# Inverse roots by Newton steps on GpSimd, and the interval layer's right products on two row tiles

## The chip, the cores and the metric

The kernel runs on one core of a Trainium2 chip. The metric is the device time of one execution in microseconds, taken as the median of several runs; one more execution was profiled.

## The reference

Input `x` is a batch of 4 images of 32x32 pixels with 16 channels. Three pre-activation layers of one kind and one of another are applied, each as `x = x + layer(gn(x))`, where `gn` is a group norm with 8 groups of 2 channels:

```python
def _gn(v, G=8, eps=1e-5):
    g = v.reshape(B_, H_, W_, G, C_ // G)
    m = jnp.mean(g, axis=(1, 2, 4), keepdims=True)
    s = jnp.var(g, axis=(1, 2, 4), keepdims=True)
    return ((g - m) / jnp.sqrt(s + eps)).reshape(v.shape)
...
# the three conv layers (L0, L1, L3)
first = jnp.einsum('ijyx,byxc->bijc', Msq, inputs)
diff = jax.nn.relu(inputs[:, None, None] - shifted)   # shifted: a 3x3 convolution for every pixel
second = jnp.einsum('ijyx,bijyxc->bijc', Wsq, diff)
return first - second
...
# the interval layer (L2), between the second and the third conv layer
r = interval_pooling(a, 'max') and interval_pooling(a, 'min'), side by side
ft = einsum('bikd,dh->bikh', f, Wf);  rt = einsum('bkjd,dh->bkjh', r, Wr)
f = max over k of sigmoid(ft + rt + b)    # twice, then a last sigmoid(f @ W2 + b2)
```

The convolution in a conv layer has its own 3x3 kernel for each of 1024 pixels and 16 output channels. That is nearly all of the arithmetic.

## The kernel before

The two halves of the batch (`g` = 0, 1; two images each) and the three conv layers make six phases, numbered in the order (layer 0, g 0), (layer 0, g 1), (layer 1, g 0) and so on. A phase has 8 chunks of 128 pixels, and a chunk has 32 steps: 16 channels times 2 images. There are 1536 steps. One step makes one PSUM tile `pc` of 128 pixels by 1024 positions:

- `first_part` (products at L627, tiles `ib` and `ia`) writes it, and ScalarE scales it at L663.
- `second_part` of the step before is issued after that (products at L627, tiles `iyz` and `im`), and then VectorE reduces that tile into one column at L680 (`junk`, the line that frees the tile).

So TensorE's order is first part of step n+1, second part of step n, first part of step n+2, and so on. The PSUM pool holds four pairs of banks, and `pc` tiles take them in turn. A product contracts 64 rows, and the two halves of a tile use two row tiles of TensorE, the partitions 0 to 63 and 64 to 127, one bank of the pair each.

Two other strands are woven into the steps, and the order on each engine is that of the program text, since each engine works through its own queue.

The generator `prep_parts` prepares the weights, one unit of four channels in 8 steps: VectorE takes the upper bits (L203, `upper_w`, which reads `raw` after L214), ScalarE scales and copies (L175, L236, L240), GpSimd (POOL in the profile) subtracts and adds and moves quarters (L237, L238, L241, L243, L245) and subtracts an identity from the next unit's `raw` (L214). Then SP's queue issues the transfer of `parts` (L251) and the load of a `raw` two units ahead (L110).

The generator `behind(phase)` does all that the next phase needs: the group norm, the images in the arrangement of the taps, the first terms `pf` (L425) and the interval layer. Each `yield n` in it gives the number of steps until it is resumed; `yield IDLE` waits for a step in which `prep_parts` allows it.

`group_norm` sums on VectorE, spreads the totals over the partitions (`totals`; its last instruction is the transpose to `whole_v...` at L337), takes the root on ScalarE (L358) and the reciprocal on VectorE (L360), and multiplies on GpSimd (L361, into `xn` for a conv layer and `xi` for the interval layer). Ahead of it a Sqrt of one element (`spare`, L353) loads ScalarE's table. There are eight norms: six named `c` for the conv layers and two named `i` for the interval layer. Afterwards VectorE transposes the result (L375 for `xn`, L508 for `xi`).

`interval_layer` fills a table `r` of 64 rows by 33x33 by scans and selects (the last select is L538), and then in each of two `step`s needs a left product (L548, `ps_l`) and a right product (L561, `ps_r`). `right_side` makes the right product in three blocks of 11 values of `k`, with 352, 231 and 110 columns. Each block has a PSUM tile of its own, and a copy by ScalarE into `rt` (L564) and one step lie between two blocks. Each `step` ends in a Sigmoid, ahead of which a Sigmoid of one element (L591) loads the table.

Of the kernel before, what the change touches and what calls it, by code (L numbers as in the profile page):

```python
# [8 lines left out]
F32 = mybir.dt.float32  # L9
F32R = mybir.dt.float32r  # L10
I32 = mybir.dt.int32
AF = mybir.ActivationFunctionType
ALU = mybir.AluOpType
AX = mybir.AxisListType

P = 128
B, H, C = 4, 32, 16
NG = 2
GB = B // NG
GC = GB * C  # L20
NL = 3
NP = H * H
# [16 lines left out]
T1 = H + 1  # L39
NQ = 4  # L40
# [4 lines left out]
def net_kernel(ctx: ExitStack, tc: tile.TileContext, x, xq, xi, convs, iv_w, iv_b, out):  # L45
# [26 lines left out]
    nc = tc.nc  # L72
    ctx.enter_context(tc.manual_schedule())

    const = ctx.enter_context(tc.tile_pool(name="const", bufs=1))
    wpool = ctx.enter_context(tc.tile_pool(name="wpool", bufs=2))
    work = ctx.enter_context(tc.tile_pool(name="work", bufs=1))
# [5 lines left out]
    def bank_pair(name):  # L83
        return psum.tile([P, 2, 512], F32, tag="ps", name=name)

    def bank(name):
        return bank_pair(name)[:, 0]
# [10 lines left out]
    IDLE = 0  # L98
# [55 lines left out]
    spare = const.tile([1, 1], F32, name="spare")  # L154
    nc.gpsimd.memset(spare, 0.0)
    eps = const.tile([P, 1], F32, name="eps")
# [152 lines left out]
    def pair_view(ap):  # L309
        return ap.rearrange("p t (g s) -> p t g s", s=2)  # L310

    def group_norm(g, name, dst, gap):


        def sums(src):
            nc.vector.tensor_reduce(
                part[:, : GC // 2], src.rearrange("p t (g s) -> p g t s", s=2), axis=AX.XY, op=ALU.add
            )

        def totals(name):  # L320

            turned = work.tile([P, 32], F32, tag="turned", name=f"turned_{name}")
            nc.vector.transpose(turned, part)
            by_quarter = work.tile([32, 4], F32, tag="by_quarter", name=f"by_quarter_{name}")
            for q in range(4):
                nc.vector.tensor_reduce(
                    by_quarter[:, q : q + 1], turned[32 * q : 32 * q + 32], axis=AX.X, op=ALU.add
                )
            yield gap
            total = work.tile([P, 32], F32, tag="total", name=f"total_{name}")  # L330
            for q in range(4):
                nc.vector.tensor_reduce(
                    total[32 * q : 32 * q + 32, 0:1], by_quarter, axis=AX.X, op=ALU.add
                )
            yield gap
            whole = work.tile([P, 32], F32, tag="whole", name=f"whole_{name}")
            nc.vector.transpose(whole, total[:, 0:1].to_broadcast([P, 32]))  # L337
            return whole[:, : GC // 2]

        sums(X[g])  # L340
        yield gap
        m = yield from totals(f"m{name}")
        mean = work.tile([P, GC // 2], F32, tag="mean", name=f"mean_{name}")
        nc.gpsimd.tensor_scalar_mul(mean, m, 1.0 / (2 * NP))
        xc = work.tile([P, NT, GC], F32, tag="xc", name=f"xc_{name}")
        nc.gpsimd.tensor_tensor(pair_view(xc), pair_view(X[g]), spread(mean), ALU.subtract)
        sq = work.tile([P, NT, GC], F32, tag="sq", name=f"sq_{name}")
        nc.gpsimd.tensor_tensor(sq, xc, xc, ALU.mult)
        yield 4
        sums(sq)  # L350
        yield gap
        yield IDLE
        nc.scalar.activation(spare, spare, AF.Sqrt)  # L353
        v = yield from totals(f"v{name}")
        yield 2
        yield IDLE
        rstd = work.tile([P, GC // 2], F32, tag="rstd", name=f"rstd_{name}")
        nc.scalar.activation(rstd, v, AF.Sqrt, bias=eps, scale=1.0 / (2 * NP))  # L358
        yield 2
        nc.vector.reciprocal(rstd, rstd)  # L360
        nc.gpsimd.tensor_tensor(pair_view(dst), pair_view(xc), spread(rstd), ALU.mult)  # L361
        yield 3

# [54 lines left out]
    def first_terms(layer, mt):  # L418


        sums = bank_pair(f"pf_{layer}")
        for g in range(NG):
            for pt in range(NT):
                for j in range(4):
                    nc.tensor.matmul(  # L425
                        sums[32 * j : 32 * j + 32, g, :256],
                        lhsT=xns[g][:, pt, :], rhs=mt[:, pt, j, :],
                        start=pt == 0, stop=pt == NT - 1, tile_position=(0, 32 * j),
                    )
        ft = work.tile([P, NG, NT * GC], F32, tag="fs", name=f"ft_{layer}")  # L430
        for g in range(NG):
            nc.vector.transpose(ft[:, g], sums[:, g, : NT * GC])
        yield 1
        for g in range(NG):
            nc.vector.tensor_tensor(
                X[g], X[g], ft[:, g].rearrange("p (t m) -> p t m", t=NT), ALU.add
            )
            yield 1


    rt = const.tile([P, T1, T1], F32, name="rt")
# [4 lines left out]
    def constants():  # L446
        nc.sync.dma_start(wv, iv_w)
        nc.sync.dma_start(bv, iv_b)
        mask2 = const.tile([P, GB], F32, name="mask2")
        nc.vector.tensor_reduce(  # L450
            mask2, ident.rearrange("p (s b c) -> p b s c", b=GB, c=C), axis=AX.XY, op=ALU.add
        )

        nc.gpsimd.tensor_scalar_mul(mask2[GC : 2 * GC], mask2[GC : 2 * GC], -1.0)
        yield 2

        def blocks(dst, k, mask, n, p0=0):
            p = dst.shape[0]
            nc.gpsimd.tensor_tensor(
                dst,  # L460
                wv[p0 : p0 + p, k, :].unsqueeze(1).to_broadcast([p, n, C]),
                mask[p0 : p0 + p].unsqueeze(2).to_broadcast([p, n, C]),
                ALU.mult,
            )

        nc.gpsimd.memset(rt, 0.0)
        yield 1


        for k, hidden, name in ((0, None, "f0"), (3, 2, "f1"), (6, 5, "f2")):  # L470
            n = 64 if hidden is None else 96
            t = const.tile([n, GB, C], F32, name=name)
            blocks(t[:64], k, mask2, GB)
            if hidden is not None:
                blocks(t[64:], hidden, mask2, GB, 64)
            iv[name] = t.rearrange("p k c -> p (k c)")
            yield 1
        for k, name in ((1, "r0"), (4, "r1")):
            t = const.tile([64, NQ * GB, C], F32, name=name)
            for q in range(NQ):  # L480
                blocks(t[:, q * GB : (q + 1) * GB, :], k, mask2, GB)
            iv[name] = t.rearrange("p k c -> p (k c)")
            yield 1
    def interval_layer(g):

        R = 2 * GC
        xi = ivp.tile([P, NT, GC], F32, tag="xi", name=f"xi_{g}")
        tables = big.tile([P, 8192], F32, tag="big", name=f"tables_{g}")
        n = H * H
# [32 lines left out]
        def running(dst, src):  # L522
# [16 lines left out]
            out=r[:R, :H, 1:], in_=table(one), pattern=[[-1, H], [1, H]], compare_op=ALU.is_ge,  # L539
            fill=0.0, base=0, channel_multiplier=0,  # L540
        )
        yield 5

        def left(name, wf):
# [9 lines left out]

        def right_side(name, wr):

            for k0 in range(0, T1, 11):
                j0 = k0 + 1
                ps = bank(f"ps_{name}{g}{k0}")
                n = T1 - j0  # L560
                nc.tensor.matmul(  # L561
                    ps[:, : 11 * n], lhsT=wr, rhs=r[:R, k0 : k0 + 11, j0:], start=True, stop=True
                )
                nc.scalar.copy(  # L564
                    rt[:, j0:, k0 : k0 + 11],
                    ps[:, : 11 * n].rearrange("p (k j) -> p j k", j=n),
                )
                yield 1

        def step(name, ftp, bias):  # L570

            ft = ivp.tile([P, QI, T1], F32, tag="ft", name=f"ft_{name}{g}")
            nc.scalar.copy(ft, ftp)
            yield 2
            s = ivp.tile([P, QI, T1], F32, tag="s", name=f"s_{name}{g}")
            last = None
            for i in range(QI + 1):
                if i < QI:
                    t = dp[i % 2]
                    nc.gpsimd.tensor_tensor(  # L580
                        t,
                        ft[:, i, :].unsqueeze(1).to_broadcast([P, T1, T1]),
                        rt,
                        ALU.add,
                    )
                if last is not None:
                    nc.vector.tensor_reduce(s[:, i - 1, :], last, axis=AX.X, op=ALU.max)
                last = t
                yield 6 if i < QI else 3
            yield IDLE  # L590
            nc.scalar.activation(spare, spare, AF.Sigmoid)  # L591
            yield 2
            yield IDLE
            nc.scalar.activation(s, s, AF.Sigmoid, bias=bias)
            for q in range(NQ):
                nc.sync.dma_start(r[R:, QI * q : QI * (q + 1), :], s[GC * q : GC * (q + 1)])
            yield 4
# [8 lines left out]
        y = ivp.tile([P, QI, H], F32, tag="y", name=f"y_{g}")  # L606
# [373 lines left out]
```

## Time and profile before

| | us |
|---|---|
| median of 3 runs | 2477.86 (2477.18 to 2479.97) |
| profiled execution | 2478.41 |
| its span, first to last instruction | 2476.7 |
| TensorE busy | 2458.2 (99%) |
| VectorE busy | 2087.3 (84%) |
| ScalarE busy | 1878.4 (76%) |
| GpSimd busy | 1579.7 (64%) |

The groups of the profile give a line of the kernel, the engine, the operation, what it writes and reads, the busy time and the mean duration of one, and the idle time of the engine before it with what ended that. The timeline gives the start in us from the start of the span, the duration, and in brackets the idle time before. Several like instructions in a row are merged with their number. A product in full fp32 appears as two records, one for each pass.

### The profile page before, as it was taken

Reading aid. Unit: us, or ns where it says so; the run is one execution under the profiler, and the core shown is the slowest. Engines: PE = TensorE matmul, PEld = TensorE weight load, DVE = VectorE, ACT = ScalarE, POOL = GpSimd, SP = SyncE. Lnnn points to the kernel's source line nnn. Section 1 sums busy time; section 2 is a strip of 40 time slices with the busy share of each in tenths; the row PEclk is TensorE's granted clock in tenths of the full one; section 3 lists DMA queues with packets and bytes.
Section 4 is the critical chain, followed back from the end, with each engine's and each line's share of the span. In section 5 each row is a group of like instructions: output and inputs, shape, how many; then the busy total and the mean of one; then the engine's idle time right before and its main releaser. Section 6 shows DMA issues by size and latency. Waiting matters only on the chain.

```text
span 2476.7 us, 58058 instructions
## 1 busy us (share of the span) xinstructions
PE 2458.2 (99%) x21906; PEld 2090.1 (84%) x21906; DVE 2087.3 (84%) x3617; ACT 1878.4 (76%) x2181; POOL 1579.7 (64%) x1750
## 2 busy tenths in 40 slices
PE   8999999999999999999999999999999999999999
PEld 5999888888888888888888988888998888888887
DVE  9888878888888888778898988899889888788887
ACT  4778767787777778777777777787777787677776
POOL 4766655666565657555567777586878676555552
PEclk9999999999999999999999999999999999999999
DMA  6446754466454467644454545574455467554442
GB/s 198 138 137 182 203 155 135 124 182 164 133 143 135 135 168 198 186 116 134 136 145 127 142 124 140 146 196 125 126 138 144 127 181 195 154 148 137 137 137 54
DMA packets 97673, 366.92 MB, mean 148 GB/s; under 512 B 26480, under 2 KB 31472, under 8 KB 97392
## 3 DMA queue, kind: packets, MB, share of 16 engines
q1 hardware_dynamic: 96832, 362.79, 53.0%
q8 instruction: 172, 2.82, 0.5%
q14 instruction: 109, 0.89, 0.1%
q10 hardware_dynamic: 432, 0.39, 0.1%
q0 software_dynamic: 128, 0.02, 0.0%
HBM read 199.78 MB, written 1.02 MB: 81 GB/s over the span
## 4 chain that ended last, share of the span: by engine, by line
PE 94%; DVE 2%; issue 1%; DMA 1%; ACT 0%; SPq 0%; POOL 0%; ACTq 0%; DVEq 0%; POOLq 0%
PE pc L627 93%; DVE junk L680 1%; PE pf L425 1%; DMA raw<-in_g 1%; ACT pc L663 0%; DMA first<-in_g 0%; SPq L298 0%; DVE raw L846 0%; SPq L300 0%; PE ps_l L548 0%; PE ps_r L561 0%; DMA parts<-parts 0%; DVE tables L508 0%; DVE raw L854 0%; DMA ib<-first 0%
## 5 line engine op out<-in xcount | busy, mean ns | idle before, releaser
L680 DVE SCALAR_TENSOR_TENSOR junk<-pc,WT 128x1024 f32<-128x1024 f32 x1536 | 1879.5, 1224 | 359.1 <-PE pc L627 308.3
L663 ACT ACTIVATE pc<-pc 128x1024 f32<-128x1024 f32 x1520 | 1532.0, 1008 | 561.0 <-PE pc L627 535.8
L627 PE MATMUL pc<-ib,parts 64*128 64x512 f32 x6080 | 958.5, 388 | 4.1 <-DVE junk L680 3.4
L627 PE MATMUL pc<-iyz,parts 64*128 64x512 f32 x6080 | 955.5, 387 | 2.2 <-ACT pc L663 2.0
L627 PE MATMUL pc<-ia,parts 64*128 64x496 f32 x6080 | 933.5, 379 | 0.0
L627 PEld LDWEIGHTS pc<-ia,parts 64*128 64x128 f32 x6080 | 595.5, 184 | 100.8
L627 PEld LDWEIGHTS pc<-ib,parts 64*128 64x128 f32 x6080 | 591.5, 184 | 105.0 <-DVE junk L680 9.9
L627 PEld LDWEIGHTS pc<-iyz,parts 64*128 64x128 f32 x6080 | 592.5, 184 | 88.4 <-ACT pc L663 6.4
L627 PE MATMUL pc<-im,W 64*128 64x496 f32 x3072 | 611.5, 384 | 0.0
L237 POOL TENSOR_TENSOR parts<-raw,upper_w 128x512 fp32r<-128x512 f32 x190 | 248.5, 1308 | 500.2 <-DVE upper_w L203 434.8
L627 PEld LDWEIGHTS pc<-im,W 64*128 64x128 f32 x3072 | 303.0, 184 | 54.5 <-issue 3.2
L243 POOL CAST parts<-parts 32x512 fp32r<-32x512 f32 x380 | 231.1, 608 | 50.1 <-ACT parts L240 31.8
L238 POOL TENSOR_TENSOR W<-W,raw 128x512 fp32r<-128x512 f32 x190 | 247.6, 1303 | 1.8 <-ACT W L175 1.8
L241 POOL TENSOR_TENSOR parts<-parts 128x512 fp32r<-128x512 f32 x190 | 246.8, 1299 | 2.0 <-ACT parts L236 1.9
L245 POOL CAST parts<-upper_w 32x512 fp32r<-32x512 f32 x380 | 231.6, 609 | 22.8
L214 POOL TENSOR_TENSOR raw<-raw,ident 128x512 f32<-128x512 f32 x190 | 199.9, 1052 | 52.2 <-DMA raw<-in_g 28.7
L175 ACT ACTIVATE W<-raw,low_w 128x512 fp32r<-128x512 f32 x190 | 136.2, 717 | 0.1
L680 DVE DVE_READ_ACCUMULATOR junk<-pc,WT 128x1 f32 x1536 | 127.5, 83 | 0.0
L236 ACT ACTIVATE parts<-upper_w 128x512 fp32r<-128x512 f32 x190 | 118.8, 625 | 6.6 <-DVE upper_w L203 6.4
L240 ACT CAST parts<-upper_w 128x512 fp32r<-128x512 f32 x190 | 116.5, 613 | 0.0
L695 POOL TENSOR_SCALAR acc<-acc 128x32 f32<-128x32 f32 x40 | 16.4, 409 | 141.7 <-DVE junk L680 139.7
L203 DVE TENSOR_SCALAR upper_w<-raw 128x512 int32<-128x512 int32 x190 | 86.1, 453 | 1.2 <-POOL raw L214 0.9
(139 smaller groups left out, 479.4 us busy)
## 6 DMA issues: line engine op xcount, KB each, us to landing
raw<-in_g SPq DMA_DIRECT2D x190, 768.0 KB, 7.1
parts<-parts SPq DMA_DIRECT2D x380, 384.0 KB, 4.9
WT<-in_w SPq DMA_DIRECT2D x48, 512.0 KB, 4.6
MT<-in_mt SPq DMA_DIRECT2D x24, 512.0 KB, 7.4
raw<-xs SPq DMA_DIRECT2D x120, 71.8 KB, 2.9
ib<-temp SPq DMA_DIRECT2D x40, 128.0 KB, 2.6
ia<-temp SPq DMA_DIRECT2D x80, 62.0 KB, 3.4
ib<-first SPq DMA_DIRECT2D x8, 128.0 KB, 2.4
```

Of the source, the lines that this page charges most:

```text
L175: nc.scalar.activation(dst, src, AF.Copy, scale=mask[:, 1:2])
L214: eng.tensor_tensor(raws[u][:, s, at:to], raws[u][:, s, at:to], pick[s][:, f0 + at : f0 + to].unsqueeze(2).to_broadcast([P, to - at, P]), ...
L236: nc.scalar.activation(WD, high, AF.Copy, scale=-EPS)
L237: nc.gpsimd.tensor_tensor(WL, w8, high, ALU.subtract)
L238: nc.gpsimd.tensor_tensor(W9, W9.bitcast(F32), src[:, 2], ALU.add)
L240: nc.scalar.copy(WU, high)
L241: nc.gpsimd.tensor_tensor(WD, WD.bitcast(F32), WL.bitcast(F32), ALU.add)
L243: nc.gpsimd.tensor_copy(WU[hi], WL[lo].bitcast(F32))
L245: nc.gpsimd.tensor_copy(WL[lo], high[hi])
L627: nc.tensor.matmul(ps[:, h, at : at + n], lhsT=w[r], rhs=v[r] if n == NH else v[r][:, :n], start=first and k == 0, stop=k == len(pairs) - ...
L663: nc.scalar.activation(ps, ps, AF.Copy, scale=1.0 + EPS)
L680: nc.vector.scalar_tensor_tensor(junk, ps.rearrange("p h n -> p (h n)"), 0.0, chunks[n], op0=ALU.min, op1=ALU.mult, accum_out=accs[phase][ ...
```

## The change

The inverse root of the variance is taken by four Newton rounds on GpSimd, from a start value that VectorE makes by two integer operations. ScalarE has no Sqrt any more after the start, so the Sqrts of one element and the Sigmoids of one element in the steps go; one Sigmoid of one element stands in `first_terms` of layer 0. The pauses between the root's parts sum to those before.

In the interval layer the table `r` is copied to the partitions 64 to 127 by GpSimd (`below`). The weights `r0` and `r1` have 128 partitions instead of 64, and a second product with -1 gives the mask its lower half. `right_side` issues its three products together into one PSUM tile: the block of 352 columns from the upper rows into one bank, those of 231 and 110 columns from the lower rows into the other bank. The three copies into `rt` follow with one step between them.

On TensorE, ScalarE and VectorE nothing else changes places. On GpSimd, the root's instructions are queued where the program text has them. In the conv norms of layers 0 and 1 the first two stand right behind L214. In the two norms of the interval layer and in the conv norms of layer 2 they stand between an L214 and the L237 of the next unit; the first round comes after L238, the second after the casts L243 and L245, and the third and the fourth after the next L214, ahead of L361.

```diff
+    def inverse_root(v, name):
+        n = GC // 2
+        a, y, t = (
+            work.tile([P, n], F32, tag=tag, name=f"{tag}_{name}") for tag in ("root_a", "root_y", "root_t")
+        )
+        nc.gpsimd.tensor_scalar(a, v, 1.0 / (2 * NP), 1e-5, op0=ALU.mult, op1=ALU.add)
+        nc.vector.tensor_scalar(
+            t.bitcast(I32), a.bitcast(I32), 1, None, op0=ALU.logical_shift_right
+        )
+        nc.vector.tensor_scalar(
+            y.bitcast(I32), t.bitcast(I32), -1.0, float(0x5F3759DF), op0=ALU.mult, op1=ALU.add
+        )
+        nc.gpsimd.tensor_scalar_mul(a, a, -0.5)
+        for pause in (1, 1, IDLE, 2):
+            yield pause
+            nc.gpsimd.tensor_tensor(t, a, y, ALU.mult)
+            nc.gpsimd.tensor_tensor(t, t, y, ALU.mult)
+            nc.gpsimd.tensor_scalar(t, t, 1.5, None, op0=ALU.add)
+            nc.gpsimd.tensor_tensor(y, y, t, ALU.mult)
+        return y
...
         yield IDLE
-        nc.scalar.activation(spare, spare, AF.Sqrt)
         v = yield from totals(f"v{name}")
-        yield 2
-        yield IDLE
-        rstd = work.tile([P, GC // 2], F32, tag="rstd", name=f"rstd_{name}")
-        nc.scalar.activation(rstd, v, AF.Sqrt, bias=eps, scale=1.0 / (2 * NP))
-        yield 2
-        nc.vector.reciprocal(rstd, rstd)
+        rstd = yield from inverse_root(v, name)
         nc.gpsimd.tensor_tensor(pair_view(dst), pair_view(xc), spread(rstd), ALU.mult)
...
+        if layer == 0:
+            nc.scalar.activation(spare, spare, AF.Sigmoid)
...
-        nc.gpsimd.tensor_scalar_mul(mask2[GC : 2 * GC], mask2[GC : 2 * GC], -1.0)
+        for at in (GC, 3 * GC):
+            nc.gpsimd.tensor_scalar_mul(mask2[at : at + GC], mask2[at : at + GC], -1.0)
...
-            t = const.tile([64, NQ * GB, C], F32, name=name)
+            t = const.tile([P, NQ * GB, C], F32, name=name)
...
+        below = tables[R:, : T1 * T1].rearrange("p (i j) -> p i j", j=T1)
+        nc.gpsimd.tensor_copy(below, r[:R])
+        tops = (r[:R], below)
         yield 5
...
-            for k0 in range(0, T1, 11):
+            ps = bank_pair(f"ps_{name}{g}")
+            blocks = []
+            for k0, h, at in ((0, 0, 0), (11, 1, 0), (22, 1, 11 * (T1 - 12))):
                 j0 = k0 + 1
-                ps = bank(f"ps_{name}{g}{k0}")
                 n = T1 - j0
+                blocks.append((k0, j0, n, ps[:, h, at : at + 11 * n]))
                 nc.tensor.matmul(
-                    ps[:, : 11 * n], lhsT=wr, rhs=r[:R, k0 : k0 + 11, j0:], start=True, stop=True
+                    blocks[-1][3], lhsT=wr[R * h : R * h + R], rhs=tops[h][:, k0 : k0 + 11, j0:],
+                    start=True, stop=True,
                 )
+            for k0, j0, n, sums in blocks:
                 nc.scalar.copy(
-                    rt[:, j0:, k0 : k0 + 11],
-                    ps[:, : 11 * n].rearrange("p (k j) -> p j k", j=n),
+                    rt[:, j0:, k0 : k0 + 11], sums.rearrange("p (k j) -> p j k", j=n)
                 )
                 yield 1
...
-            nc.scalar.activation(spare, spare, AF.Sigmoid)
             yield 2
             yield IDLE
             nc.scalar.activation(s, s, AF.Sigmoid, bias=bias)
```

## The prediction

> **What bounds the kernel.** I read the chain that ended last, then the groups, then the timeline engine by engine around each edited place.
>
> ```profile
> PE 94%; DVE 2%; issue 1%; DMA 1%; ACT 0%; SPq 0%; POOL 0%; ACTq 0%; DVEq 0%; POOLq 0%
> ...
> L680 DVE SCALAR_TENSOR_TENSOR junk<-pc,WT 128x1024 f32<-128x1024 f32 x1536 | 1879.5, 1224 | 359.1 <-PE pc L627 308.3
> ```
>
> TensorE (PE) is the bound: 94% of the chain. One step is one `pc` tile: its last products (`im`) follow each other every 1.567 us. Only two things move the end: fewer PE columns, or fewer (or more) stalls of PE behind the other engines. Each step's DVE work (1.22 plus 0.08 us, one every 1.37 us when DVE is behind) regains 0.2 us a step. A stall can be sized from one place before: the `junk` at 1287.61 started 2.43 us after its `im` row (1285.17); two steps on, the distance between `im` rows was 2.06 (1288.31 to 1290.37), 0.50 too long. The reason is that PE needs the bank pair back which that `junk` reads, four `pc` tiles later. So DVE may start about 1.93 us behind `im` before PE pays; in rest it is 0.48 behind.
>
> **Right sides.** One of the four, before:
>
> ```profile
> 1434.22 0.38 PE L627 MATMUL pc<-im,W 64*128 64x496 f32 x2
> 1435.79 0.38 PE L627 MATMUL pc<-im,W 64*128 64x496 f32 x2
> 1436.01 0.45 PE L561 MATMUL ps_r<-tables,r 64*128 64x352 f32 x1
> 1436.01 0.48 PE L627 MATMUL pc<-ib,parts 64*128 64x512 f32 x1
> 1436.30 0.45 PE L561 MATMUL ps_r<-tables,r 64*128 64x352 f32 x1
> ...
> 1437.98 0.38 PE L627 MATMUL pc<-im,W 64*128 64x496 f32 x1
> ```
>
> The step with the 352-column block takes 2.19 instead of 1.57: 0.62 over. The next two (231 and 110 columns) are 0.42 and 0.24 over. For `r0` (1327.75 on) it is 0.75, 0.42, 0.26. All four sum to 2 x (0.62+0.42+0.24+0.75+0.42+0.26) = 5.4 us. The change puts 231+110 columns on the lower row tile beside the 352 on the upper one, so the first excess stays and the second and third go: 2 x (0.66+0.68) = 2.7 us. The Trainium skill, TensorEngine Tiling (Array Packing), Key Properties, says that different tiles can load weights and multiply in parallel. The rows agree: a `pc` product starts on the other tile at 1436.01, with the first `ps_r` pass and ahead of its second. I go by the row. Against this, one PSUM pair stays taken over three steps, so PE's free margin falls by a step to 1.93-1.57 = 0.36, while DVE is 0.48 behind: about 0.1 a side. Gain 2.3 us; none if the tiles take turns.
>
> The new copy `below` on GpSimd has 64x1089 elements: 1.3 us by the 608 ns cast of 512 columns, at most the 2.2 us of the strided L534 copy. It stands after the select that ended at 1323.04; the product needing it comes at 1328, and GpSimd idled 3.65 us afterwards. Nothing on the path; without that idle time it would cost its own length. The other additions (one mask row, 128 partitions for 64) are 0.2 us once, beside PE work.
>
> **Table loads.** Four leave, one comes.
>
> ```profile
> L591 ACT ACT_TABLE_LOAD  x2: 1283/1283/1283, 1420.2 to 1831.9; - x2
> L353 ACT ACT_TABLE_LOAD  x2: 1283/1283/1283, 1564.0 to 1975.7; - x2
> 1422.63 0.73 PE L627 MATMUL pc<-iyz,parts 64*128 64x512 f32 x4 [0.39 <-ACT pc L663]
> ```
>
> The skill's ScalarE: Activation LUTs, What ACT_TABLE_LOAD costs, gives 1.28 us plus a drain, 2.66 us in all. The trace gives less: one `pc` ended at 1564.02, the next began at 1565.44, so 1.42 us; I use the trace. What counts is PE's loss: the step with L591's load was 2.23 long, 0.67 over (0.66 the second time): 1.3 us gained. L353's loads cost 0.67 each too, counted below. The new load stands behind the first-term products `pf`, 7.04 us in which ScalarE has no `pc` to scale: nothing; 0.7 us if that cover were missing. The removed Sqrts fall into 0.56 us idle gaps: nothing.
>
> **Roots.** GpSimd gets 18 small instructions a norm. No row has 128x16 with two inputs; near are
>
> ```profile
> L344 POOL TENSOR_SCALAR mean_c<-whole_mc 128x16 f32<-128x16 f32 x6 | 1.5, 253 | 18.6 <-DVE whole_mc L337 18.4
> L459 POOL TENSOR_TENSOR r<-wv,mask 64x32 f32<-64x32 f32 x8 | 1.6, 230 | 0.1
> L696 POOL TENSOR_TENSOR X<-X,acc 128x32 f32<-128x32 f32 x40 | 10.2, 254 | 3.3
> ```
>
> and 0.08 us between dependent ones (3.3/40). A Newton round is 3x0.23+0.253+3x0.08 = 1.18 us; bounds 0.9 (0.15 for the small product, my estimate) to 1.4 (all rows 0.25 to 0.29, four gaps).
>
> What matters is the order. `root_a` waits for `whole_v`, and GpSimd's queue behind it waits too. In the four norms of layers 0 and 1 GpSimd ended L214 0.3 us after `whole_v` and then waited up to 7.6 us for the root; the rounds fit in there. DVE waits for `root_a` and does two instructions: `junk` starts 0.9 us late, 1.4 behind, under 1.93. Cost nothing; past 1.93, what exceeds it.
>
> In layer 2 (two interval norms, two conv norms) the weights' preparation was in that place:
>
> ```profile
> 1269.62 1.30 POOL L237 TENSOR_TENSOR parts<-raw,upper_w 128x512 fp32r<-128x512 f32 x1 [5.45 <-DVE upper_w L203]
> 1276.18 1.04 POOL L214 TENSOR_TENSOR raw<-raw,ident 128x512 f32<-128x512 f32 x1
> 1279.30 0.68 POOL L361 TENSOR_TENSOR xi<-xc_i,rstd_i 128x256 f32<-128x256 f32 x1 [2.08 <-DVE rstd_i L360]
> ...
> 1283.67 1.31 DVE L508 STREAM_TRANSPOSE tables<-xi 32x256 f32<-32x256 f32 x2
> ```
>
> L237 had run before `whole_vi` ended (1272.11). Now it stands behind `root_a`. From 1272.11: hand-over 0.09 (rstd to `xi`), `root_a` 0.25, DVE's first instruction and hand-overs 0.3, the -0.5 product 0.25: L237 at 1273.0, 3.4 us later. L237 and L238 2.5, round 1.18, L241 1.3, four casts 2.65, round 1.18, L214 with its gap 1.12: L214 ends at 1282.95 (was 1277.22). DVE's L203 for the next unit reads that `raw` and was due at 1280.54: 2.4 us late, with every `junk` behind it. Two rounds 2.44 and `xi` 0.76: `xi` ends at 1286.15, and L508 starts at 1286.2 instead of 1283.67. The `junk` that was already 2.43 behind comes 2.5 us later, all of it beyond the margin. DVE's wait at `root_a` itself (0.75 at a `junk` 1.04 behind, 1.8) is under it. Loss 2.5 us, twice: 5.0.
>
> Conv norm of layer 2: `whole_vc` ends 1569.71, L237 had begun at 1566.77. The same sum puts L214's end at 1580.5 (was 1575.17), L203 at 1580.55 (was 1578.18) and `xn` at 1583.7, before L375 that stood at 1581.31. The `junk` behind it starts at 1584.2 against `im` at 1581.25: 2.97 behind, 1.0 beyond. That is net of the 0.67 that leave with L353's load, since DVE's and GpSimd's own times there don't move. Loss 1.0, twice: 2.0. On SP's queue the `parts` and `raw` transfers go out about 5 us later; they have a unit (12.5 us) and more, so nothing; without that cover up to their 5 us would show.
>
> **Sum.** -2.3 -1.3 +5.0 +2.0 = +3.4 us on 2478.41 (span 2476.7 and 1.7 around it), so 2481.8 for a profiled execution; the median before is 0.55 lower, so 2481.3. A measurement can tell about 0.2%, 5 us: no difference below 2482.8.
>
> **Rivals.** (a) The rounds are longer: each 0.1 us more an operation is 0.4 a round, 1.6 a norm, 6.4 over four. It decides from 0.1 us: from there the sum is over 5 us; at that price 2487.7. For it: dependent chains of tiny GpSimd work hardly occur in the trace. Against: L344 is the very shape, at 0.25. (b) GpSimd's delay is absorbed, because its queue is not held at `root_a` or DVE catches up: only the gains stay, with L353's 0.7 each: -2.3-1.3-1.4 = -5.0, 2472.9. Against: L203 reads `raw`, a real dependence, and DVE has 0.2 us a step. (c) The row tiles take turns, so that part doesn't do what it says: +5.7, 2483.6. Against: the 1436.01 rows.
>
> **Chances.** Main case 0.65, a fifth of it beyond 5 us, since rounds of 0.9 or 1.4 us give +0.8 or +6.4; (a) 0.19; (b) 0.10; (c) 0.06. Slower 0.13+0.19+0.06 = 0.38; faster 0.04, near half of (b); same 0.58. Range: the main case's 2478.7 to 2484.3, widened to (a) and partly to (b): 2475.0 to 2487.5.
>
> **What would show it.** `ps_r` passes of 352 and 231 columns side by side, and two steps of 1.57 to 1.7 after the first; no table load after the first interval layer begins; L203 waiting for POOL's L214 about 2 us and L508 for `xi` in both interval norms; `im` rows there losing 3 us. If L203 and L508 wait for nothing, the forecast fails towards (b); if rounds exceed 1.3 us, towards (a).

## The result, and the profile after

The changed kernel takes 2483.15 us (median of 17 runs, 2481.43 to 2484.59); the kernel before took 2478.60 us beside it (2475.52 to 2481.25). The ratio is 1.0019 with a 95% interval of 1.0012 to 1.0027: 4.55 us slower, just under the 0.2% that the forecast named as the least that a measurement can tell. The forecast was 3.4 us slower, which made 2481.3 for the median.

The page of the changed kernel, first its span and busy times, then the chain that ended last, then the group of `junk` (busy time, mean ns | idle time before it):

```profile
span 2481.2 us, 58191 instructions
PE 2458.0 (99%) x21906; PEld 2085.2 (84%) x21906; DVE 2088.1 (84%) x3625; ACT 1871.5 (75%) x2159; POOL 1613.8 (65%) x1897
...
PE 90%; DVE 3%; POOL 3%; DMA 2%; issue 2%; SPq 1%; ACT 0%; ACTq 0%; DVEq 0%; POOLq 0%
...
L704 DVE SCALAR_TENSOR_TENSOR junk<-pc,WT 128x1024 f32<-128x1024 f32 x1536 | 1879.5, 1224 | 349.8 <-PE pc L651 293.0
```

TensorE's busy time has not moved (2458.2 before). ScalarE lost 7 us, GpSimd gained 34, and neither shows in the end. What moved is the chain: PE holds 90% of it instead of 94%, and GpSimd, VectorE, transfers and SyncE's queue (SP) have taken the rest. So the whole difference is stalls of PE.

I size them by steps. A place is a stretch of a few steps, and its entry is the time between the first and the last `im` row of that stretch (of a step's two `im` products, the later one), less the same time in the kernel before. The names of the experiments are explained below; "g0" and "g1" are the two halves of the batch.

| us against before | right sides, all 4 | L591, 2 loads | interval norms g0, g1 | conv norms of layer 2 g0, g1 (net of L353) | the transfers behind those g0, g1 |
|---|---|---|---|---|---|
| forecast | -2.3 | -1.3 | +2.5, +2.5 | +1.0, +1.0 | 0, 0 |
| after | -2.27 | -1.39 | +2.27, +2.27 | +0.81, +0.91 | +0.50, +1.26 |
| e1 roots only | -0.11 | -1.40 | +2.27, +2.27 | +0.81, +0.95 | +0.95, +1.16 |
| e2 right sides only | -2.21 | 0.00 | -0.02, -0.04 | -0.03, +0.05 | -0.11, +0.24 |
| e3 start on VectorE | -2.27 | -1.40 | +0.01, +0.01 | -0.28, +0.05 | +0.45, +0.01 |
| e4 one row tile | +0.01 | -1.39 | +2.25, +2.25 | +0.85, +0.92 | +0.45, +0.69 |
| e5 three rounds | -2.27 | -1.39 | +1.90, +1.95 | +0.79, +0.93 | +0.95, +1.23 |
| e6 start on VectorE, loads back | -2.16 | -0.01 | 0.00, -0.01 | -0.03, +0.16 | 0.00, +0.07 |
| e7 start on VectorE, later | -2.21 | -1.39 | +0.49, +0.50 | -0.11, -0.12 | -0.01, +0.14 |
| e8 all rounds behind L214 | -2.30 | -1.39 | +3.23, +3.44 | +1.17, +1.25 | +0.75, +0.97 |
| e9 conv norms on VectorE | -2.23 | -1.39 | +2.27, +2.26 | -0.29, -0.26 | +0.10, -0.09 |
| e10 interval norms on VectorE | -2.19 | -1.39 | -0.04, -0.02 | +0.85, +0.88 | +0.99, +0.93 |

The entries of one column repeat to about 0.1 us wherever the code of that place is the same (to 0.3 at the conv norm of g1, e3 against e9); the last column, where transfers land, to 0.5. The rest of a profiled execution (mainly the first steps, and the landing of images and weights elsewhere) differs by up to 4 us from one execution to the next, so I compare places within traces and medians of many runs, and no two spans.

**The interval norm.** The timeline of the changed kernel, first GpSimd, then VectorE:

```profile
1270.89 0.20 POOL L318 TENSOR_SCALAR root_a_i<-whole_vi 128x16 f32<-128x16 f32 x1 [8.04 <-DVE whole_vi L359]
1271.39 0.25 POOL L325 TENSOR_SCALAR root_a_i<-root_a_i 128x16 f32<-128x16 f32 x1 [0.29 <-DVE root_t_i L319]
1271.60 1.30 POOL L237 TENSOR_TENSOR parts<-raw,upper_w 128x512 fp32r<-128x512 f32 x1
...
1280.42 1.04 POOL L214 TENSOR_TENSOR raw<-raw,ident 128x512 f32<-128x512 f32 x1
...
1283.97 0.67 POOL L377 TENSOR_TENSOR xi<-xc_i,root_y_i 128x256 f32<-128x256 f32 x1
...
1281.49 0.43 DVE L203 TENSOR_SCALAR upper_w<-raw 128x512 int32<-128x512 int32 x1 [2.01 <-POOL raw L214]
...
1284.68 1.30 DVE L527 STREAM_TRANSPOSE tables<-xi 32x256 f32<-32x256 f32 x2 [0.25 <-POOL xi L377]
```

PE stood 1.31 us earlier here than in the kernel before (from differences in earlier steps), so 1.31 is to be added before times are compared. L237 then starts at 1272.91 (forecast 1273.0; before, 1269.62), L214 ends at 1282.77 (1282.95), `xi` at 1285.95 (1286.15), and the transpose starts at 1285.99 (1286.2; before, 1283.67). The 8.04 us in the first row are GpSimd idle with L237 queued behind the waiting `root_a`; L237 itself started 3.3 us later than before. VectorE waits twice in this place, 2.01 us at L203 and then 0.25 us more at the transpose. The transpose is 2.32 us late, and PE lost 2.27.

**Right sides.** Groups by form, with busy time and mean ns:

```profile
L585 PE MATMUL ps_r<-tables,r 64*128 64x352 f32 x8 | 3.0, 455 | 0.0
L585 PE MATMUL ps_r<-tables,r 64*128 64x231 f32 x8 | 2.2, 358 | 0.0
L585 PE MATMUL ps_r<-tables,r 64*128 64x110 f32 x8 | 1.5, 262 | 0.0
```

Each pass is as long as before (454, 357 and 261 ns), and the step that holds all three is no longer than the one that held the 352 columns alone (2.19 both times, in the second right side). The next two steps take 1.60 and 1.65 us instead of 1.99 and 1.81.

**Table loads and the small GpSimd work**, the same view:

```profile
L447 ACT ACT_TABLE_LOAD x1 | 1.3, 1283 | 0.0
...
L562 POOL COPY tables<-tables 64x1089 f32<-64x1089 f32 x2 | 2.2, 1094 | 0.1
...
L328 POOL TENSOR_TENSOR root_t_i<-root_a_i,root_y_i 128x16 f32<-128x16 f32 x8 | 1.8, 220 | 0.3
L330 POOL TENSOR_SCALAR root_t_i<-root_t_i 128x16 f32<-128x16 f32 x8 | 2.0, 254 | 0.7
```

The new load among the first terms costs nothing (that step is 8.84 us in both kernels). The copy `below` takes 1.09 us, and the trace shows nobody who waits for it. A round is 220 + 236 + 254 + 224 ns and three gaps of 0.08: 1.17 us.

**What the forecast did not have.** The chain that ended last, in order of time, behind the first conv norm of layer 2:

```profile
1587.25 1.88 DMA xs<-xt
...
1594.29 0.02 SPq L251
...
1594.91 6.41 DMA parts<-parts
1601.32 0.04 issue
1601.37 2.77 PE pc L651 x17
```

PE waits until 1601.37 for weights' parts. They stood in SyncE's queue behind the copies of the late `xn`, and then took 6.41 us to land. How much is due to each comes with e9 and e10.

### The profile page after: what moved, and what is told of

Read it like the earlier page. It is cut to its first block, busy times and chain, and to the rows that moved or that the text cites. A ratio compares the mean times of both kernels' runs of the same rounds, so it can differ in the third digit from the quotient of the medians.

```text
span 2481.2 us, 58191 instructions
## 1 busy us (share of the span) xinstructions
PE 2458.0 (99%) x21906; PEld 2085.2 (84%) x21906; DVE 2088.1 (84%) x3625; ACT 1871.5 (75%) x2159; POOL 1613.8 (65%) x1897
## 4 chain that ended last, share of the span: by engine, by line
PE 90%; DVE 3%; POOL 3%; DMA 2%; issue 2%; SPq 1%; ACT 0%; ACTq 0%; DVEq 0%; POOLq 0%
PE pc L651 89%; DVE junk L704 2%; PE pf L441 1%; DMA raw<-in_g 1%; SPq L408 0%; DMA parts<-parts 0%; POOL parts L241 0%; POOL parts L245 0%; POOL parts L243 0%; POOL parts L237 0%; SPq L397 0%; POOL raw L214 0%; DMA first<-in_g 0%; POOL W L238 0%; DVE raw L870 0%
## 5 line engine op out<-in xcount | busy, mean ns | idle before, releaser
L651 PEld LDWEIGHTS pc<-ia,parts 64*128 64x128 f32 x6080 | 589.5, 184 | 102.2
L237 POOL TENSOR_TENSOR parts<-raw,upper_w 128x512 fp32r<-128x512 f32 x190 | 248.4, 1307 | 474.0 <-DVE upper_w L203 414.0
L243 POOL CAST parts<-parts 32x512 fp32r<-32x512 f32 x380 | 231.1, 608 | 46.8 <-ACT parts L240 27.8
L238 POOL TENSOR_TENSOR W<-W,raw 128x512 fp32r<-128x512 f32 x190 | 247.6, 1303 | 1.5 <-ACT W L175 1.5
L245 POOL CAST parts<-upper_w 32x512 fp32r<-32x512 f32 x380 | 231.6, 610 | 22.8
L214 POOL TENSOR_TENSOR raw<-raw,ident 128x512 f32<-128x512 f32 x190 | 199.5, 1050 | 51.8 <-DMA raw<-in_g 21.4
L203 DVE TENSOR_SCALAR upper_w<-raw 128x512 int32<-128x512 int32 x190 | 86.3, 454 | 9.0 <-POOL raw L214 8.6
```

The source lines that it names most:

```text
L214: eng.tensor_tensor(raws[u][:, s, at:to], raws[u][:, s, at:to], pick[s][:, f0 + at : f0 + to].unsqueeze(2).to_broadcast([P, to - at, P]), ...
L237: nc.gpsimd.tensor_tensor(WL, w8, high, ALU.subtract)
L238: nc.gpsimd.tensor_tensor(W9, W9.bitcast(F32), src[:, 2], ALU.add)
L243: nc.gpsimd.tensor_copy(WU[hi], WL[lo].bitcast(F32))
L245: nc.gpsimd.tensor_copy(WL[lo], high[hi])
L651: nc.tensor.matmul(ps[:, h, at : at + n], lhsT=w[r], rhs=v[r] if n == NH else v[r][:, :n], start=first and k == 0, stop=k == len(pairs) - ...
```

## The experiments

The theory was that GpSimd's queue, held at `root_a` for the sum of squares, pushes the weights' preparation and the scaled output back, and that VectorE's waits for these are what costs. The rivals were those of the prediction: longer rounds, and row tiles that take turns.

**e1 and e2: each half alone.** e1 keeps the new root and undoes the right side:

```diff
-        below = tables[R:, : T1 * T1].rearrange("p (i j) -> p i j", j=T1)
-        nc.gpsimd.tensor_copy(below, r[:R])
...
-            ps = bank_pair(f"ps_{name}{g}")
...
+                ps = bank(f"ps_{name}{g}{k0}")
```

> The changed kernel with the right side of the kernel before (three tiles, three steps, no copy of the table). My theory (GpSimd's queue held at root_a in layer 2): the gain of the right sides, 2.2 to 2.3 us, is missing, so about 4.6 + 2.3 = +7 us against the kernel before (+0.28%), with the same losses of 2.3 us in each interval norm and 0.7 to 0.9 us in each conv norm of layer 2. Rival (the two-tile right side and its copy on GpSimd cost, not the roots): +2 us or less.

Measured: 2487.35 us (5 runs), ratio 1.0036 (1.0023 to 1.0049): +8.6. The interval and conv norms lose what they lose in the changed kernel, and the right sides gain nothing.

e2 is the opposite, the right side alone with the old root (and the one-element Sqrts and Sigmoids back in their places):

```diff
-        rstd = yield from inverse_root(v, name)
+        yield 2
+        yield IDLE
+        rstd = work.tile([P, GC // 2], F32, tag="rstd", name=f"rstd_{name}")
+        nc.scalar.activation(rstd, v, AF.Sqrt, bias=eps, scale=1.0 / (2 * NP))
+        yield 2
+        nc.vector.reciprocal(rstd, rstd)
```

> The kernel before with the right side of the changed kernel alone; roots and table loads as before. My theory: -2.2 us against the kernel before (-0.09%): in each of four right sides the second and third steps lose their 0.42 and 0.25 us and get about 0.1 back from the pair that stays taken. Rival (the taken pair or the late copy eats it): 0 or above, with junk waits of 0.4 us or more in these steps.

Measured: 2476.38 us (13 runs), 0.9990 (0.9981 to 0.9998): -2.4. The two halves add up to +6.1 from single medians, against +4.55; their places in the table add up within 0.2 but for the last column.

**e4: one row tile.** All three products on the upper rows:

```diff
-                    blocks[-1][3], lhsT=wr[R * h : R * h + R], rhs=tops[h][:, k0 : k0 + 11, j0:],
+                    blocks[-1][3], lhsT=wr[:R], rhs=tops[0][:, k0 : k0 + 11, j0:],
```

> The changed kernel with the third right product of the interval side put on the upper 64 rows as well, as if the lower row tile didn't exist for it (it then reads the upper table rows, so its values are other ones; the work is the same in size). If the gain of the right sides comes from two row tiles working at once, the second and third steps of each right side lose what they had gained: +0.5 to +0.6 in each, four times +0.55, 2.2 us over the changed kernel, about 2485.3. If it came from the other reshaping of that part (one table of 128 partitions, the copy in front), the steps stay as in the changed kernel and the time is 2483.1.

The edit moves both lower products, where that text speaks of the third alone; and the lower rows hold copies, so the values are the same, unlike what it says. Measured: 2486.81 us (5 runs), 1.0030 (1.0018 to 1.0043). The changed kernel's gain of 2.27 is gone to the last hundredths (+0.01). But it is lost elsewhere than I expected: the second and third steps stay short (1.60 and 1.66), and the first one grows from 2.19 to 2.80. The timeline of PE:

```profile
1437.89 0.38 PE L651 MATMUL pc<-im,W 64*128 64x496 f32 x2
1438.11 1.15 PE L585 MATMUL ps_r<-tables,r 64*128 64x352 f32 x4
1438.91 0.50 PE L651 MATMUL pc<-ib,parts 64*128 64x512 f32 x1
1439.11 0.36 PE L585 MATMUL ps_r<-tables,r 64*128 64x110 f32 x2
...
1440.69 0.39 PE L651 MATMUL pc<-im,W 64*128 64x496 f32 x1
```

The three blocks follow each other on one tile (the first row holds the passes of 352 and of 231 columns), while a `pc` product goes ahead on the other at 1438.91. So the gain is the second row tile, and grouping the products alone gives nothing.

**e5: three Newton rounds.** The fourth round is left out, so the root is less exact:

```diff
         for pause in (1, 1, IDLE, 2):
             yield pause
+            if pause == 2:
+                continue
```

> The changed kernel with three Newton rounds instead of four; the start on GpSimd as changed. My theory (two waits end together in the interval norms: L203 for L214, behind root_a, two rounds and the weights; and the transpose for xi, behind two more rounds): only the second gets shorter, by 1.2 us, and it was 0.25 us the later one, so each of the four norms of layer 2 gains 0.25 us or a little more: about +3.5 us against the kernel before instead of +4.5. Rival (the length of the rounds sets the loss): 1.2 us gained in each of four norms, +4.5 - 4.8 = about 0.

Measured: 2484.10 us (12 runs), 1.0022 (1.0013 to 1.0030), no faster than with four. Each interval norm loses 0.32 to 0.37 us less, and the conv norms nothing less. Its VectorE shows why:

```profile
1283.94 0.43 DVE L203 TENSOR_SCALAR upper_w<-raw 128x512 int32<-128x512 int32 x1 [2.01 <-POOL raw L214]
...
1286.79 1.30 DVE L529 STREAM_TRANSPOSE tables<-xi 32x256 f32<-32x256 f32 x2
```

The transpose waits for nothing any more, but L203 waits 2.01 us as in the changed kernel, since L214 still stands behind the hold and two rounds. So L203's wait by itself costs 1.90 to 1.95 us at an interval norm, and the transpose's adds the rest. The fourth round is a small part of what is lost.

**e3: the start on VectorE.** GpSimd's two instructions at the start go to VectorE, so that nothing on GpSimd waits for the sum of squares ahead of L237:

```diff
-        nc.gpsimd.tensor_scalar(a, v, 1.0 / (2 * NP), 1e-5, op0=ALU.mult, op1=ALU.add)
+        nc.vector.tensor_scalar(a, v, 1.0 / (2 * NP), 1e-5, op0=ALU.mult, op1=ALU.add)
...
-        nc.gpsimd.tensor_scalar_mul(a, a, -0.5)
+        nc.vector.tensor_scalar_mul(a, a, -0.5)
```

> The changed kernel with root_a and its product with -0.5 on VectorE instead of GpSimd, so that GpSimd's queue is not held until whole_v is there and VectorE does not wait for GpSimd; the 16 instructions of the rounds stay on GpSimd. My theory (the hold costs, not the rounds): L237 of the next unit runs before whole_v as in the kernel before, L214 ends about 2.3 us later than there and still ahead of L203, xi about 2.9 us later and still ahead of its transpose; no loss in the four norms of layer 2, so -2.2 (right sides) -1.3 (loads of the steps) -1.4 (loads in the conv norms) = -5 us against the kernel before (-0.2%). Rival (the rounds themselves are too long for GpSimd): the losses of the interval norms shrink by a third at most, and it stays at +2 us or above.

Measured: 2475.48 us (13 runs), 0.9987 (0.9979 to 0.9996). All 16 GpSimd instructions of the rounds are still there, and the interval norms lose 0.01 us. Its timeline, VectorE and then GpSimd:

```profile
1270.23 0.17 DVE L318 TENSOR_SCALAR root_a_i<-whole_vi 128x16 f32<-128x16 f32 x1
...
1281.75 1.31 DVE L527 STREAM_TRANSPOSE tables<-xi 32x256 f32<-32x256 f32 x2
...
1270.97 0.22 POOL L328 TENSOR_TENSOR root_t_i<-root_a_i,root_y_i 128x16 f32<-128x16 f32 x1 [0.72 <-DVE root_a_i L325]
```

GpSimd waits 0.72 us in place of 8.04, L203 and the transpose wait for nothing. The rounds' work alone costs nothing at the interval norms; it takes the hold to make L214 and `xi` late. At the conv norms of layer 2, 0.39 and 0.67 us remain in the step where the four instructions come; VectorE is behind there. This version beats both kernels.

**e8: which of VectorE's two waits costs.** The hold stays, but all four rounds go behind L214:

```diff
-        for pause in (1, 1, IDLE, 2):
-            yield pause
+        yield 2
+        for pause in (IDLE, None, None, 2):
+            if pause is not None:
+                yield pause
```

> The changed kernel with the start still on GpSimd (so its queue is still held for the sum of squares), but all four rounds behind the L214 product. L214 then ends 2.4 us sooner and L203 should wait for nothing or little, while the scaled output comes no sooner than in the changed kernel, since all four rounds are ahead of it. If what costs is the transpose's wait for the scaled output, VectorE's loss is the same: 2.3 us at each interval norm, about 1 at each conv norm of layer 2, 2483 in all. If what costs is L203's wait, with everything queued behind it on VectorE, the interval norms lose 0.5 or less each and the whole is 2479 to 2480.

Measured: 2487.07 us (6 runs), 1.0030 (1.0019 to 1.0042), worse than the changed kernel. VectorE's timeline:

```profile
1280.82 0.42 DVE L203 TENSOR_SCALAR upper_w<-raw 128x512 int32<-128x512 int32 x1
...
1286.49 1.26 DVE L529 STREAM_TRANSPOSE tables<-xi 32x256 f32<-32x256 f32 x2 [2.63 <-POOL xi L379]
```

L203 waits for nothing now, though the hold is still there: the hold alone fits into the slack of L214, as the rounds alone did in e3, and it takes both to make L203 wait. Yet the norm loses 3.2 to 3.4 us instead of 2.27. Together with e5 this says that either wait is enough to cost: with L203's alone the norm loses 1.9, with the transpose's alone 3.2 or more. What L203 no longer waits, the transpose does, and what counts is how late VectorE gets through both: the transpose starts 2.0 us late in e5, 2.32 in the changed kernel and 2.7 here. My size was too low by 1 us a norm, since `xi` came 0.4 later and the one long pause brought a new cost. TensorE in stretches of time (length, busy time, PEclk, DMA share, GB/s):

```profile
1284.00:1287.00 3.00, 3.00 (x30) 1.00 0.77 270
1287.00:1289.00 2.00, 0.22 (x4) 1.00 0.02 7
1289.00:1290.50 1.50, 1.43 (x8) 0.68 0.00 0
1290.50:1292.00 1.50, 1.50 (x10) 0.50 0.00 0
1292.00:1294.00 2.00, 2.00 (x17) 0.76 0.07 15
```

After a pause of 1.85 us the granted clock was at half for 3.4 us (0.96 + 1.5 + 0.96 from the last three rows, taking it as either full or half). The other interval norm of this run shows the same. After the three pauses of 0.44, 0.73 and 0.72 us in the changed kernel it stayed at 1.00.

**e7: the start on VectorE, two steps later.** Where VectorE has caught up; rounds one and two then stand directly ahead of L214, three and four behind it:

```diff
+        yield 2
+        nc.vector.tensor_scalar(a, v, 1.0 / (2 * NP), 1e-5, op0=ALU.mult, op1=ALU.add)
...
-        for pause in (1, 1, IDLE, 2):
-            yield pause
+        for pause in (None, None, IDLE, 2):
+            if pause is not None:
+                yield pause
```

> The root's start on VectorE, two steps later than in the version before this one, where VectorE has caught up; rounds one and two then stand directly ahead of the L214 product on GpSimd and three and four behind it. My theory: no engine's queue is held for the sum of squares any more, and the losses of 0.39 and 0.67 us at the conv norms of layer 2 go: about 2474.4, 4.4 under the kernel before, and no step of the interval norms longer than before. The rival, that the sheer GpSimd time of the rounds (4.7 us a norm) costs something wherever it stands: two rounds ahead of L214 delay L203 by 2.4 us and the step there loses 0.5 to 2.

Measured: 2476.52 us (21 runs), 0.9991 (0.9985 to 0.9998): a gain of 2.2 instead of 4.4. About 0.45 us is lost at each of the four norms, but not by the rival, since no VectorE instruction waits for GpSimd's rounds. VectorE, and then GpSimd, in the first interval norm:

```profile
1275.31 0.61 DVE L320 TENSOR_SCALAR root_t_i<-root_a_i 128x16 int32<-128x16 int32 x1
1275.95 0.64 DVE L323 TENSOR_SCALAR root_y_i<-root_t_i 128x16 int32<-128x16 int32 x1
...
1275.28 1.27 POOL L245 CAST parts<-upper_w 32x512 fp32r<-32x512 f32 x2
```

The same two instructions take 0.17 us in e3, where GpSimd is idle. Here they end at 1275.92 and 1276.59, and GpSimd's two casts ended at 1275.88 and 1276.56. From the first start to the last end the four instructions take 1.55 us of VectorE instead of 0.67. The Trainium skill has the rule, in SBUF — State Buffer, Who interferes with whom: VectorE's `tensor_scalar` can take the port pair that it shares with GpSimd, and the one that comes second is fully blocked. The rows agree. In e3 the layers 0 and 1 show it too: `root_a` beside an L214 takes 0.31 to 0.60 us.

**e6: the price of the table loads.** e3 with the four loads back in their places (the Sigmoids of the steps likewise, and none among the first terms):

```diff
         yield IDLE
+        nc.scalar.activation(spare, spare, AF.Sqrt)
         v = yield from totals(f"v{name}")
...
+            nc.scalar.activation(spare, spare, AF.Sigmoid)
```

> The version with the root's start on VectorE, and the ScalarE table loads put back where the kernel before had them (a one-element Sqrt ahead of the conv norms' totals and a one-element Sigmoid in the steps; none among the first terms). The only difference to the version with the start on VectorE is four table loads of 1283 ns. My ledger: each costs PE 0.67 us, so 2.7 us over that version: about 2478.2, 0.6 under the kernel before. If a load cost the 2.66 us that the Trainium skill gives (ScalarE: Activation LUTs, What ACT_TABLE_LOAD costs), it would be 10.6 over; if the loads lay in ScalarE's slack, nothing.

Measured: 2477.94 us (13 runs), 0.9997 (0.9989 to 1.0005), 2.5 us over e3. The four steps with a load are longer by 0.66, 0.67, 0.66 and 0.67 us. So a load costs PE what the trace of before gave, and not the 2.66 us that the Trainium skill, ScalarE: Activation LUTs, What ACT_TABLE_LOAD costs, has for a switch on ScalarE. ScalarE went 1.42 us there without scaling a `pc`, and 0.56 of that is idle between two scalings anyway. At the conv norms it is not all net, though. With the load in place, the stall of 0.39 and 0.67 us that e3 has a few steps later is gone but for 0.04. By places the four loads cost 1.6 us net; the medians say 2.5, and their intervals, 2 us to either side each, don't tell these apart.

**e9 and e10: what makes the parts late.** The start on VectorE for one sort of norm alone (`"c"` in e9, `"i"` in e10):

```diff
+        eng = nc.vector if name[0] == "c" else nc.gpsimd
-        nc.gpsimd.tensor_scalar(a, v, 1.0 / (2 * NP), 1e-5, op0=ALU.mult, op1=ALU.add)
+        eng.tensor_scalar(a, v, 1.0 / (2 * NP), 1e-5, op0=ALU.mult, op1=ALU.add)
...
-        nc.gpsimd.tensor_scalar_mul(a, a, -0.5)
+        eng.tensor_scalar_mul(a, a, -0.5)
```

> The changed kernel with the root's start on VectorE for the conv norms alone; the interval norms keep it on GpSimd, which is held there. What it tells apart is the loss of 1.3 us about 19 us behind each conv norm of layer 2 (and of 1 us at the second one), where TensorE waits for weights' parts. My theory: the conv norm's output xn comes late, its xs and raw copies stand on SyncE's queue ahead of the next unit's parts, and so the parts go out late. Then these losses are gone here though the interval norms still lose 2.3 us each: 2475.5 + 4.6 = 2480.1. If the interval norms' hold (which delays parts and raw as well) is what makes them late, they stay: 2481.6.

> The other half: the root's start on VectorE for the interval norms alone, the conv norms held on GpSimd. My theory: interval norms lose nothing, the conv norms of layer 2 lose 1.0 us at the transpose's place as in the changed kernel (1.9 us in all over the version with every start on VectorE), and the losses behind them stay, 0.5 us net at the first and 1.0 at the second: 2475.5 + 1.9 + 1.5 = 2478.9. The rival, that the interval norms' hold is behind those: 2477.4, with no loss about 19 us behind the conv norms.

Measured: e9 2479.91 us (13 runs), 1.0007 (0.9999 to 1.0015); e10 2479.86 us (13 runs), 1.0003 (0.9994 to 1.0011). The medians do not tell the two apart; the table does. e9 keeps both interval losses and has none in the last column (+0.10, -0.09); e10 has no interval loss and keeps +0.99 and +0.93 there. So it is the conv norm's hold. SyncE's queue tells how, first in the kernel before:

```profile
1581.78 5.26 SPq L381 DMA_DIRECT2D xs<-xt  x8
1587.82 5.70 SPq L392 DMA_DIRECT2D raw<-xs  x12
1593.68 1.11 SPq L251 DMA_DIRECT2D parts<-parts  x2
```

The changed kernel:

```profile
1582.92 4.78 SPq L397 DMA_DIRECT2D xs<-xt  x8
1588.52 5.72 SPq L408 DMA_DIRECT2D raw<-xs  x12
1594.40 1.11 SPq L251 DMA_DIRECT2D parts<-parts  x2
```

And e10, with the wait of PE at the end:

```profile
1597.94 1.11 SPq L251 DMA_DIRECT2D parts<-parts  x2
...
1604.94 0.50 PE L652 MATMUL pc<-ib,parts 64*128 64x512 f32 x1 [1.25 <-DMA parts<-parts]
```

Twenty transfers of the conv norm's output stand ahead of the next unit's parts. I count from the `im` row of a step ahead of the norm's first loss (1571.85 before, 1570.01 after, 1573.14 in e10, 1569.85 in e9). L251's two transfers start after 21.83 us before, 24.39 in the changed kernel, 24.80 in e10, and 21.91 in e9 (at 1591.76): 2.56 us later in the changed kernel than before. The second of the two also takes longer to land, as L251's line shows, before and after:

```profile
DMA to landing us min/median/max: 3.9/4.6/5.3
DMA to landing us min/median/max: 3.9/5.1/6.4
```

So these parts are there 3.7 us later. Before, they had landed 1.0 us ahead of the product that needs them, and PE's own steps are 1.5 us late by then. That leaves PE 1.2 us of waiting. The step there is 1.32 too long, of which 0.82 come back four steps on. Without the 1.1 us of longer landing the parts would have come about in time, and e8 agrees: its second transfer starts nearly as late, lands in 5.3 us, and PE waits for none of it (its steps are 1.9 us late by then). The landing takes 6.4 or 6.5 us in e1, e4, e5 and e10 too, and 5.1 to 5.3 in all the others. Why it takes longer was not looked for.

In the second half PE does not wait for the parts. There the copies of the images stand still further back in the same queue, and VectorE's L203 waits for them, before and after:

```profile
2015.78 0.74 DVE L203 TENSOR_SCALAR upper_x<-raw 128x1024 int32<-128x1024 int32 x1 [0.84 <-DMA raw<-xs]
2018.93 0.69 DVE L203 TENSOR_SCALAR upper_x<-raw 128x1024 int32<-128x1024 int32 x1 [2.06 <-DMA raw<-xs]
```

The wait is 1.22 us longer, and PE loses 1.26.

## Why the prediction was right, and which step of it failed

- **The bound, the hold and the order on GpSimd** held. Every time of the interval norm that was worked out came within 0.3 us, and a hold removed (e3) removes the loss.
- **Interval norms**, +2.5 forecast: 2.27 each. L203 waits for L214 and the transposes for `xi`, as said. The forecast took the size from the transposes' lateness; e5 shows that 1.9 of it comes with L203's wait already.
- **Right sides**, -2.3: -2.27. e4 shows the second row tile to be the reason. The allowance of 0.1 a side was right in size: 0.03 and 0.08 us are left in the second and third steps. That the bank pair held over three steps is the reason was not tested.
- **L591's loads**, -1.3: -1.39, and 0.66 a load in e6. The load in `first_terms` and the `below` copy cost nothing, as said, and behind the norms of layers 0 and 1 no step lost more than 0.2 us.
- **Conv norms of layer 2**, +1.0 each: +0.81 and +0.91. L353's load gives back its 0.67 and the transpose's step loses 1.01 and 1.11. The 0.39 and 0.43 in the step where the root starts were not in the forecast.
- **The round**, 1.18 us: 1.17.
- **The step that failed** is "On SP's queue the `parts` and `raw` transfers go out about 5 us later; they have a unit (12.5 us) and more, so nothing". It looked at the transfers of the held unit, which do have cover. It left out that `xn`, whose transpose starts 3.0 us late against PE's steps, has transfers of its own, `xs` and `raw`. The *next* unit's parts stand behind these in the same queue with 1.0 us of cover (g0), and for the images in the last of them VectorE waited 0.84 us already before (g1). VectorE's slack takes 1.6 of the 3.0 us off PE's loss, while SyncE's queue makes up only 0.4. Price: +0.50 and +1.26 us, so 1.8 in this trace where 0 stood. Over the six kernels with GpSimd held at the conv norm it is 1.1 to 2.2, over the five others 0.0 to 0.5.

The places add up to -2.27 - 1.39 + 4.54 + 1.72 + 1.76 = +4.36, and -0.38 at one step of the first interval layer's scans, which every kernel with the new root has but e10 (-0.19) and whose cause was not looked for: +4.0. The medians give +4.55. What is left, 0.6 us, is no more than the landing of transfers varies. It is partly luck that the total came so near the forecast: 0.7 us that the norms cost less than forecast, and the 0.38 that nobody forecast, took back 1.1 of the 1.8 that were missed.

Of the rivals, long rounds fell with the round of 1.17 us, the row tiles that take turns fell with the trace and e4, and the absorbed delay is what e3 makes true by another edit: forecast for it -5.0, measured -3.3.

## What to carry to other kernels

Before a small instruction that waits is put on an engine that works through a queue, read what stands behind it there: here two instructions of 0.2 us held other work up for 3.3 us, and the same two on the engine that produces their input cost 0.01 us at the interval norms (0.4 to 0.7 at the conv norms of layer 2). A late result is followed to the end of its path: past the engine that reads it to the transfers that it feeds, and to what else is queued behind these. And a small instruction need not keep its price in another place: VectorE's two took 0.17 us beside an idle GpSimd and over 0.6 beside its casts, so a place is chosen with the other engine's timeline in hand.

## What was not expected of the hardware

- VectorE's small `tensor_scalar` of 0.17 us took 0.61 to 0.64 us beside GpSimd's casts of 0.61 us, and 0.31 to 0.60 beside an L214: it ends when GpSimd's instruction does. `junk`, with one operand in PSUM, kept its 1.22 us beside the same casts.
- TensorE's granted clock fell to 0.50 after a single pause of 1.85 us (e8), for 3.4 us; in the changed kernel pauses of 0.44, 0.73 and 0.72 us, the last two 2.6 us from start to start, left it at 1.00, and so did a single one of 1.18 us in e8. The Trainium skill, TensorE: Matmul & The Clock Gate, What's actually happening, has the clock go down after an idle window of about 3.4 us; here it went down after a shorter pause. One long stall can thus cost more than several short ones of nearly the same sum (1.85 against 1.89 us).
